# First image read flat for its statistics, two strips read once more, and early squares added on VectorE

## The chip, the cores and the metric

The kernel runs on one core of a Trainium2 chip. The metric is the device time of one execution in microseconds; the time of a kernel is the median of several runs. Profiles come from one profiled execution.

## The reference

Two residual blocks on eight images of 384 channels and 64 x 64 pixels, all in float32:

```
x = x + window_attention(group_norm(x))      # LayerNorm over channels, qkv, 8x8 windows, two branches
x = x + fft_feed_forward(group_norm(x))      # 1x1 conv, 8x8 real FFT filter, 3x3 depthwise conv, gated gelu, 1x1 conv

def group_norm(v):                           # 32 groups of 12 channels
    g = v.reshape(B, 32, 12, H, W)
    return ((g - mean(g, (2, 3, 4))) / sqrt(var(g, (2, 3, 4)) + 1e-5)).reshape(v.shape)
```

In the attention block the normalised image is normalised once more over the channels of each pixel (LayerNorm), then multiplied with the q, k and v weights. One branch of the heads attends in 8 x 8 windows, the other in windows shifted by four pixels. What matters here is the beginning: mean and variance of a group need the whole image before the first pixel can be normalised.

## The kernel before, in words

**Strips.** An image is worked on in eight strips of eight pixel rows. A strip is a tile of 128 partitions by 3 by 512 numbers (`strip`, 768 KB): partition p holds channels 3p to 3p+2, and each channel's eight rows of 64 pixels are 512 numbers, 2 KB in one piece in memory (`rows_of`, L67). Strips come into a ring of five buffers with the tag `x`.

**Order.** Every step of every strip is put on a list with a number that says when it is due (`at`, L260; the list at L693 to L773). The sorted list is handed to a scheduler, which may reorder instructions on an engine by its own estimates, but TensorE's matmuls stay in program order. Each engine takes its instructions in order, and so does each queue of transfers. Transfers of the steady part wait, by `in_dense_work` (L276), for a certain ScalarE instruction: the move of the first q tile out of PSUM (`qab`, L374) of the strip under way (`zs["gate"]`, L390).

**The start.** SyncE's queue issues, in this order: the eight strips of image 0 (`x_first`, L72 to L76: five in the `x` ring, three in the tiles `xn`, `ow` and `y2` that are not needed yet), the constants `cst` (L78), the raw q/k weights (`wqk_raw`, L96), and the weights `wv`, `wp`, `wi`, `wo`. ScalarE's queue issues 21 small transfers: vectors, q/k biases, filter tables. GpSimd issues 64 transfers of 2 KB for the position biases (`rpb_raw`, L154).

1. VectorE takes the statistics of each strip as it lands (`bn_stats`, L220), aggregates them (L227), and a small matmul with a constant matrix (`pm_a`, L230) averages over a group. A second one (`pv_a`, L241) leads to the standard deviation, by ScalarE and a reciprocal on VectorE (L243, L244).
2. VectorE copies the raw weights into their packed order (`pack_qk`, L114): twenty copies, and six on GpSimd, which gets odd blocks of the second branch only.
3. Strips are normalised on VectorE (`group_normal`, L308, three instructions each). The strips of image 0 that are in SBUF from the statistics (0, 1 and 2) are used from there; the rest of the image is loaded again when due (`load`, L282).
4. For the LayerNorm of a strip ScalarE squares it (`ln_square`, L313), GpSimd adds the three squares of a partition (L315, two additions of 512 numbers), and TensorE sums values and squares over the partitions (`ln_sums`, tile `ln`). Row statistics go through memory (`line`, `rs`, L336 to L338) and come back to scale the strip (L343).
5. Between the sums of strips 0 and 1 TensorE computes q/k bias products (`pb`) and centres the weights (`centre`, tile `pc`), with VectorE scaling them first (L181); then the same for v (`pv`, L181, `pc`) and for the second branch's q/k. After that the dense work starts: q/k tiles (`pq`), v (`pvv`), scores (`pS`), and so on.

TensorE's program order is thus: `pm_a`, `pv_a`, `ln` of strip 0, `pb` and `pc` of branch 0, `ln` of strip 1, `pv`, `pc` of v, `pb` and `pc` of branch 1, `pq`, ...

Of the kernel before, what the change touches and what calls it, by code (L numbers as in the profile page):

```python
# [9 lines left out]
ALU = mybir.AluOpType  # L10
# [3 lines left out]
KC = 3  # L14
# [3 lines left out]
ST = WS * SW  # L18
NS = SW // WS
# [13 lines left out]
def block_kernel(ctx: ExitStack, tc: tile.TileContext, out, x, consts, fsel, wqk, wv, bqk, bv,  # L33
                 wp, bp, lng, lnb, rpb1, rpb2, w_in, w_dw, w_out, filt):
    nc = tc.nc
# [22 lines left out]
    def strip(tag, bufs, name):  # L58
        return sb.tile([P, KC, ST], F32, tag=tag, bufs=bufs, name=name)
# [7 lines left out]
    def rows_of(img, s):  # L67

        return img[:, s * WS:(s + 1) * WS, :].rearrange("(p k) h w -> p k (h w)", k=KC)

    first_x = []
    for s in range(NS):  # L72
        tag, bufs = ("x", 5) if s < 5 else (("xn", 1), ("ow", 1), ("y2", 1))[s - 5]
        t = strip(tag, bufs, f"x_first{s}")
        nc.sync.dma_start(out=t, in_=rows_of(x[0], s))
        first_x.append(t)  # L76
    cst = cp.tile([P, N_CONST], F32, name="cst")
    nc.sync.dma_start(out=cst, in_=consts)  # L78
    ident = cst[:, C_ID:C_ID + P]
# [45 lines left out]
    for j, to, n, t, hp, of in blocks:  # L125
        nc.scalar.dma_start(out=bqk_sb[to:to + n].rearrange("p (b j) -> p b j", b=2)[:, :, j],
                            in_=bqk[of:of + n, 4 * t:4 * t + 4].rearrange("p (b i) -> p b i", b=2)[:, :, hp])
# [20 lines left out]
    for br, tab in ((0, rpb1), (1, rpb2)):  # L148
        raw = sb.tile([P, 2, 64], F32, tag="t2", bufs=3, name=f"rpb_raw{br}")
        raw_bias.append(raw)  # L150
        for h in range(4):
            half = slice(h % 2 * 64, h % 2 * 64 + 64)
            for y2 in range(WS):
                nc.gpsimd.dma_start(  # L154
                    out=raw[half, h // 2, y2 * WS:(y2 + 1) * WS],
                    in_=bass.AP(tab.tensor, h * 225 + y2 * 15, [[15, 8], [1, 8], [1, 8]]),
# [106 lines left out]
    xs, ys, y2s, qks, vs, os_, ots, x1s, zs = ({} for _ in range(9))  # L263
# [12 lines left out]
    def in_dense_work(i):  # L276


        if zs.get("gate"):
            behind(i, zs["gate"], mybir.DependencyClass.Sync, "transfer in dense work")  # L280

    def load(b, s, what):  # L282

        if b == 0 and (what == "stats" or what == "norm" and s < 3):
            xs[b, s, what] = first_x[s]
            return
        t = xs[b, s, what] = strip("x", 5, f"x_{what}_{b}_{s}")
        src = x1d[b][s] if what in ("mix", "finish") else rows_of(x[b], s)
        in_dense_work(nc.sync.dma_start(out=t, in_=src))
# [21 lines left out]
    def ln_square(b, s):  # L311
        sq = ys[b, s, "sq"] = strip("sq", 1, f"sq_{b}_{s}")
        nc.scalar.activation(sq, ys[b, s], AF.Square)  # L313
        for k in (1, 2):
            nc.gpsimd.tensor_tensor(sq[:, 0, :], sq[:, 0, :], sq[:, k, :], ALU.add)  # L315

    def ln_sums(b, s):

# [374 lines left out]
    for b in range(B):  # L693
        first = 2 * NS * b

        for s in range(NS):
            u = first - 14.84 + s if b else -10 + 0.1 * s
            at(u, load, b, s, "stats")
            at(u + (0.5 if b else 0.05), input_stats, b, s)
# [11 lines left out]
        for s in range(NS):  # L711
            u = first + 2 * s

            v = u - 4
            at(v - 0.84, load, b, s, "norm")
            at(v + 0.15, group_normal, b, s)
            at(v + 0.45, ln_square, b, s)
            at(v + 0.99, ln_sums, b, s)
            at(v + 1.35, ln_scale, b, s)
# [6 lines left out]
            for br in range(2):  # L726
                w = u + br
# [14 lines left out]
            else:  # L742
                places = [first + 2 * NS + f + (0.0 if s else 0.24) for f in (0.36, 0.44, 0.52)]
            at(int(places[0]) - 0.84, load, b, s, "add")
            for m in range(KC):
                at(places[m], project, b, s, m)
# [137 lines left out]
```

## Time and profile before

| what | us |
|---|---|
| median of 3 runs (3773.02 to 3777.32) | 3776.54 |
| the profiled execution: its time | 3773.36 |
| the profiled execution: its span | 3771.3 |
| TensorE busy | 3639.9 (97%) |
| VectorE busy | 2839.3 (75%) |
| ScalarE busy | 2379.7 (63%) |
| GpSimd busy | 438.2 (12%) |
| TensorE busy from 0 to 80 us | 28.6 |
| TensorE busy from 80 to 250 us | 168.5 |

All times within an execution count from the start of its span. TensorE's busy time is modelled from its matmuls; it says where TensorE works, not that it works at its best. The clock column of the stretches says which share of TensorE's full clock was granted.

### The profile page before, as it was taken

The page shows a single profiled execution, that of the slowest core. Times are in us where ns is not written, and L with a number is a line of the kernel's source. Part 1 is how long each engine was busy: PE and PEld are TensorE (multiplying, and loading weights), DVE is VectorE, ACT ScalarE, POOL GpSimd, SP SyncE. Part 2 cuts the span into 40 slices and gives each one's busy share as a digit, 9 for nine tenths or more (in the row PEclk, how much of TensorE's full clock was granted, in tenths as well). Part 3 has the DMA queues.
Part 4 walks back from the last instruction along what each step waited for, and adds up shares of the span by engine and source line. Part 5 has one row for each costly group of instructions (what it writes and reads, how often), then busy time and mean ns, then how long its engine had stood idle before and what let it go on. Part 6 is the DMA issues. An engine that isn't in the chain of part 4 may idle for free.

```text
span 3771.3 us, 88216 instructions
## 1 busy us (share of the span) xinstructions
PE 3639.9 (97%) x38144; PEld 2315.5 (61%) x38144; DVE 2839.3 (75%) x4601; ACT 2379.7 (63%) x3946; POOL 438.2 (12%) x776
## 2 busy tenths in 40 slices
PE   4999999999999999999999999999999999999898
PEld 2666666666666666666666656666666666666554
DVE  4554578777877687777887778877788777777898
ACT  1767676666676576665766756666676666676442
POOL 5111111111101011101101011111011111100000
PEclk9999999999999999999999999999999999999999
DMA  4222222323322233323332322322232222221422
GB/s 120 85 82 74 90 99 99 107 88 108 123 97 82 88 132 107 116 79 115 108 113 83 115 96 99 132 79 99 93 127 99 107 88 82 99 79 71 160 101 76
DMA packets 144488, 377.03 MB, mean 100 GB/s; under 512 B 12308, under 2 KB 12900, under 8 KB 144100
## 3 DMA queue, kind: packets, MB, share of 16 engines
q1 hardware_dynamic: 139952, 370.60, 27.9%
q8 instruction: 300, 4.92, 0.5%
q0 software_dynamic: 2048, 0.15, 0.1%
q10 hardware_dynamic: 2100, 0.63, 0.1%
q14 instruction: 88, 0.72, 0.1%
HBM read 270.54 MB, written 100.79 MB: 98 GB/s over the span
## 4 chain that ended last, share of the span: by engine, by line
PE 86%; DVE 5%; ACT 4%; issue 2%; DMA 2%; POOL 0%; ACTq 0%; DVEq 0%; POOLq 0%
PE pq L53 24%; PE pr L53 13%; PE pt L53 13%; PE pvv L53 12%; PE pw L53 6%; PE pS L53 3%; PE pA L53 3%; PE pz L53 3%; PE pT L56 3%; PE po L56 3%; DVE zz L653 2%; PE pf L53 2%; PE ln L53 2%; PE pc L53 1%; DMA rs<-line 1%
## 5 line engine op out<-in xcount | busy, mean ns | idle before, releaser
L653 DVE SCALAR_TENSOR_TENSOR zz<-z,dw_sb,zz 128x512 f32<-128x512 f32 x1490 | 1106.5, 761 | 189.3 <-ACT zz L647 166.5
L53 PE MATMUL pq<-y,wqk_sb 128*128 128x512 f32 x2160 | 990.3, 596 | 0.1
L53 PEld LDWEIGHTS pq<-y,wqk_sb 128*128 128x128 f32 x2160 | 402.8, 190 | 456.5 <-issue 424.7
L53 PE MATMUL pt<-wi_sb,xn 128*128 128x384 f32 x1536 | 535.2, 486 | 7.2 <-DVE x_finish L686 7.2
L53 PE MATMUL pr<-oT,wp_sb 128*128 128x512 f32 x1152 | 523.1, 592 | 1.0 <-DVE oT L517 1.0
L53 PE MATMUL pvv<-wv_sb,y 128*128 128x192 f32 x2880 | 496.0, 326 | 0.1
L53 PEld LDWEIGHTS pvv<-wv_sb,y 128*128 128x128 f32 x2880 | 471.6, 190 | 36.7 <-issue 23.4
L374 ACT ACTIVATE qab<-pq,bq_sb,cst 96x512 f32<-96x512 f32 (+1 forms) x256 | 198.0, 773 | 398.8 <-PE pq L53 397.1
L53 PEld LDWEIGHTS pt<-wi_sb,xn 128*128 128x128 f32 x1536 | 286.1, 190 | 212.9 <-issue 48.6
L374 ACT ACTIVATE kcd<-pq,vec 32x512 f32<-32x512 f32 x512 | 348.9, 681 | 9.0
L53 PEld LDWEIGHTS pr<-oT,wp_sb 128*128 128x128 f32 x1152 | 211.1, 190 | 224.4 <-issue 211.6
L356 POOL COPY y<-y 128x384 f32<-128x384 f32 x112 | 100.2, 895 | 1608.0 <-PE pvv L53 1108.2
L329 DVE TENSOR_TENSOR lr<-m 128x128 f32<-128x128 f32 x64 | 19.7, 308 | 318.3 <-ACT m L327 318.3
L647 ACT ACTIVATE zz<-z,dw_sb 128x512 f32<-128x512 f32 x183 | 133.9, 733 | 192.5 <-PE pw L53 187.0
L315 POOL TENSOR_TENSOR sq<-sq 128x512 f32<-128x512 f32 x128 | 167.4, 1308 | 634.3 <-ACT sq L313 629.3
L374 ACT ACTIVATE qcd<-pq,bq_sb,cst 96x512 f32<-96x512 f32 (+1 forms) x256 | 197.3, 771 | 43.9 <-PE pq L53 40.6
L526 DVE SCALAR_TENSOR_TENSOR x_add<-pr,vec,x_add 128x512 f32<-128x512 f32 x192 | 143.6, 748 | 105.6 <-PE pr L53 103.8
L564 ACT COPY t<-pt 128x384 f32<-128x384 f32 x256 | 124.9, 488 | 147.8 <-PE pt L53 145.0
L408 ACT COPY v<-pvv 128x384 f32<-128x384 f32 x256 | 121.2, 480 | 130.5 <-PE pvv L53 130.0
L53 PE MATMUL pw<-zz,wo_sb 128*128 128x512 f32 x384 | 181.9, 610 | 0.0
L374 ACT ACTIVATE kab<-pq,vec 96x512 f32<-96x512 f32 (+1 forms) x256 | 174.4, 681 | 9.0 <-PE pq L53 7.4
L449 ACT ACTIVATE e<-e 128x1024 f32<-128x1024 f32 x128 | 135.3, 1057 | 53.4 <-DVE e L443 52.0
(139 smaller groups left out, 5273.0 us busy)
## 6 DMA issues: line engine op xcount, KB each, us to landing
x_add<-in_x_dram SPq DMA_DIRECT2D x64, 768.0 KB
x1d<-x_add SPq DMA_DIRECT2D x64, 768.0 KB
x_mix<-x1d SPq DMA_DIRECT2D x64, 768.0 KB
x_finish<-x1d SPq DMA_DIRECT2D x64, 768.0 KB
out_dram<-x_finish SPq DMA_DIRECT2D x64, 768.0 KB
x_norm<-in_x_dram SPq DMA_DIRECT2D x61, 768.0 KB
x_stats<-in_x_dram SPq DMA_DIRECT2D x56, 768.0 KB
rs<-line SPq DMA_DIRECT2D x62, 256.0 KB
```

Source lines behind the costliest of these rows:

```text
L53: tc.keep_in_program_order(nc.tensor.matmul(*args, **kw))
L56: tc.keep_in_program_order(nc.tensor.transpose(*args, **kw))
L315: nc.gpsimd.tensor_tensor(sq[:, 0, :], sq[:, 0, :], sq[:, k, :], ALU.add)
L329: nc.vector.tensor_tensor(rc, m[:, 0:P], m[:, 0:P], ALU.mult)
L356: nc.gpsimd.tensor_copy(dst[:, :, :, :, 0:4], src[:, :, :, :, 4:8])
L374: return nc.scalar.activation(dst[to:to + n], pq[of:of + n], AF.Identity, bias=bias[of:of + n], scale=scale)
L408: nc.scalar.copy(v[:, 2 * g:2 * g + 2, :, 0:HD], pvv[:, 0:384].rearrange("p (g h d) -> p g h d", g=2, h=4))
L449: nc.scalar.activation(e, e, AF.Exp)
L526: nc.vector.scalar_tensor_tensor(t[:, m, :], pr, bp_sb[:, m:m + 1], t[:, m, :], ALU.add, ALU.add)
L564: nc.scalar.copy(t1, pt[:, 0:C])
L647: nc.scalar.activation(zz.rearrange("p (r c) -> p r c", c=SW), z[:, 1:9, 1:SW + 1], AF.Copy, scale=dw_sb[:, m, 4:5])
L653: i = nc.vector.scalar_tensor_tensor(acc.rearrange("p (r c) -> p r c", c=SW), z[:, dy:dy + 8, dx:dx + SW], dw_sb[:, m, TAPS[tap]:TAPS[tap] ...
```

## The change

The image is read for its statistics in eight flat parts: part i of partition p is the i-th piece of 6 KB of its three channels, one piece in memory instead of three rows of 2 KB. The statistics do not depend on which numbers of a channel group stand together. The parts lie in `xn`, `ow`, `y2`, `yw`, `sq` and three buffers of the `x` ring; the order of a flat part isn't that of a strip, so it can't be normalised from there. Strips 0 and 1 are read once more, into the other two buffers of the ring, ahead of the constants and weights on SyncE's queue. Strip 2 is no longer kept from the statistics and is loaded when due, like strips 3 to 7. The additions of squares of the first three strips of image 0 move from GpSimd to VectorE.

```diff
     first_x = []
-    for s in range(NS):
-        tag, bufs = ("x", 5) if s < 5 else (("xn", 1), ("ow", 1), ("y2", 1))[s - 5]
-        t = strip(tag, bufs, f"x_first{s}")
-        nc.sync.dma_start(out=t, in_=rows_of(x[0], s))
+    flat = x[0].rearrange("(p k) h w -> p (k h w)", k=KC)
+    for i in range(NS):
+        tag, bufs = (("xn", 1), ("ow", 1), ("y2", 1), ("yw", 1), ("sq", 1), ("x", 5), ("x", 5), ("x", 5))[i]
+        t = strip(tag, bufs, f"x_flat{i}")
+        nc.sync.dma_start(out=t.rearrange("p k c -> p (k c)"), in_=flat[:, i * KC * ST:(i + 1) * KC * ST])
         first_x.append(t)
+    norm_x = []
+    for s in range(2):
+        norm_x.append(strip("x", 5, f"x_norm_0_{s}"))
+        nc.sync.dma_start(out=norm_x[s], in_=rows_of(x[0], s))
     cst = cp.tile([P, N_CONST], F32, name="cst")
...
     def load(b, s, what):
 
-        if b == 0 and (what == "stats" or what == "norm" and s < 3):
-            xs[b, s, what] = first_x[s]
+        if b == 0 and (what == "stats" or what == "norm" and s < 2):
+            xs[b, s, what] = (first_x if what == "stats" else norm_x)[s]
             return
...
         for k in (1, 2):
-            nc.gpsimd.tensor_tensor(sq[:, 0, :], sq[:, 0, :], sq[:, k, :], ALU.add)
+
+            eng = nc.vector if b == 0 and s < 3 else nc.gpsimd
+            eng.tensor_tensor(sq[:, 0, :], sq[:, 0, :], sq[:, k, :], ALU.add)
```

## The prediction

> **What bounds the kernel now.** First the page: TensorE is busy for 97% of the span, so a change outside its work can only pay where TensorE stands still.
>
> ```profile
> PE 3639.9 (97%) x38144; PEld 2315.5 (61%) x38144; DVE 2839.3 (75%) x4601; ACT 2379.7 (63%) x3946; POOL 438.2 (12%) x776
> PE   4999999999999999999999999999999999999898
> POOL 5111111111101011101101011111011111100000
> ```
>
> Only the first of the forty slices (94 us each) has TensorE at 4 tenths, and there GpSimd has its highest digit. So I cut that slice into 20 us stretches; the columns are PE, PEld, DVE, ACT, POOL, clock, DMA share, GB/s.
>
> ```profile
> 20.00:40.00 20.00, 2.77 (x28) 1.61 (x28) 14.17 (x45) 1.75 (x2) 13.89 (x26) 1.00 1.03 319
> 40.00:60.00 20.00, 8.60 (x32) 5.72 (x32) 5.11 (x12) 2.16 (x3) 14.55 (x42) 1.00 0.08 6
> ```
>
> From 40 to 51 us everything rests except GpSimd, and the DMA engines have nothing to carry. The waits up to 100 us name the two stalls that matter:
>
> ```profile
> PE pm_a L53 <- DVE mv_a L227: 31.9, 1, 31.9
> DVE st L220 <- DMA x_first<-in_x_dram: 15.1, 8, 5.2
> PE ln L53 <- POOL sq L315: 14.7, 1, 14.7
> ```
>
> The first two are the read of the image for its statistics. The third is the one to look at: TensorE waits 14.7 us for the two additions of the first strip's squares on GpSimd. The chain of waits says why they are late:
>
> ```profile
> 41.20 6.63 POOL rpb_raw L154 x12
> 48.47 1.30 POOL sq L315
> 49.78 0.36 POOL wqk_sb L118 x2
> 50.13 1.23 POOL sq L315
> 51.40 0.66 PE ln L53 x8
> 52.06 3.93 PE pb L53 x18
> ```
>
> GpSimd issues the 64 small bias transfers first (until 47.8 us), then clears borders, and only then adds. ScalarE had the squares ready at 37.48 (L313: start 36.00, 1.48 long). Between 37 and 51 us TensorE is bound by a queue, not by data.
>
> **What the Trainium skill says.** (1) "SBUF — State Buffer", Who interferes with whom: a VectorE instruction with two SBUF inputs and a GpSimd instruction that reads SBUF exclude each other for a whole instruction. The trace agrees: L330 takes 1.26 us at 64.42, inside GpSimd's additions of 64.27 to 66.87, but 0.28 us at 57.11, after those of 53.96 to 56.72. (2) "DMA: Bandwidth & Descriptors", Issuing engines are not separate DMA queues: all share the same engines, so what stands ahead on SyncE's queue delays what follows. The trace agrees: the constants and weights came only after the strips. (3) The same page, Latency and other measured facts, has slower copies where rows lie at large power-of-two pitches; its pitches start at 512 KiB, ours are 16 and 48 KiB, so only the direction carries over. The trace shows it: two strips in 2 KB rows alone (116.9 to 122.6 us) moved at 273 GB/s, two in 6 KB runs (3554.9 to 3563.4) at 366. (4) "TensorE: Matmul & The Clock Gate", Part 1: the clock is halved until TensorE has been busy for a few microseconds. The trace agrees: 0.50 granted from 66 to 78 us.
>
> **Part 1: the additions on VectorE.** Removed from the path: the wait 36.68 to 51.40. Price of one: the nearest row is the 128x512 float32 addition from SBUF to SBUF at L670.
>
> ```profile
> L670 DVE TENSOR_TENSOR zz<-zz,zz 128x512 f32<-128x512 f32 x63 | 43.5, 690 | 5.7 <-DVE zz L653 0.5
> ```
>
> Two take 1.38 us instead of 2.6 on GpSimd. They queue on VectorE with the scaling of strips 0 and 1 (0.55 us an instruction) and the twenty weight copies at L118 (1.22 and 1.41 us in two groups).
>
> **Part 2: the transfers.** Flat parts have 6 KB runs. Estimate for one of 786 KB: 786/366 = 2.15 us, 0.15 added for the small transfers beside it, 2.3; bounds 2.15 and the present 3.2 (statistics of strips 1 to 4 started at 10.05, 13.07, 16.29, 19.53). First bytes move at 2.2 us. SyncE also waits to issue the strips (9.8 us behind the small q/k-bias transfers, 3.9 behind a strip); most is hidden behind strips in flight, and I leave 2 us exposed. Last part landed: 2.2 + 8 x 2.3 + 2 + 0.5 = 23.1 us, against 29.1 now. Its statistics (1.88) and the aggregate (0.8) are done by 26.
>
> But the two strips read again go ahead of the constants that the group mean multiplies with: 2 x 786/273 = 5.8 us, then 0.49 MB of constants, 1.4 us. The mean can start at 23.1 + 5.8 + 1.4 = **30.3**, against 31.94. So of the 6 us won by the flat read about 1.6 remain: what is late next is the constants. Bounds: 27 (2.15 us a part, no exposed wait) and 36.3 (3.2 a part). The q/k weights, 2 x 2.15 later, are in at 34.6, about as now (their copies ran from 35.89).
>
> **Part 3: the chain behind the mean.** From mean to strip 0 scaled takes 4.03 us (31.94 to 35.97): 34.3. Square: 35.9. VectorE meanwhile does the first copies and one scaling (1.8 us, to 36.1), then the additions, to 37.5. The last eight sums on TensorE start at 37.6 (51.40 now) and take 0.66. The q/k-bias products need the second group of copies, 37.5 + 1.41 = 38.9. They start at **38.9** instead of 52.06: 13.2 us. If VectorE's order has the additions behind all copies and scalings instead, about 2 us less.
>
> **Part 4: no more exclusion.** At 65.15 TensorE waits 1.99 us for `wv_sb`, because L330 (1.26 for 0.28) and the two L181 behind it (1.82 for 0.82) ran beside GpSimd's additions. These are gone: 1.9 us.
>
> **Part 5: strip 2.** It was in SBUF; now it has one load of its own, placed after the first q move, so SyncE holds it until ScalarE's `qab` (81.52 now, about 66.5 then) and it lands about 5.5 us later (issue 0.6, latency 2, transfer 2.9), at 72. Behind it on SyncE stand only the row statistics of strip 2, due after it anyway. VectorE's scaling (3 x 0.54) and additions (1.38) move into the dense part, 3.0 us, covered by VectorE's 10.85 us idle before 108.74; without that cover they would cost 3.0. ScalarE's square (1.48) moves from an idle place (62.71) to a stretch where ScalarE has 15 of 20 us busy: bounds 0 and 1.5, I take 0.7. TensorE asks for strip 2's sums at 107.26 now, about 93 then: 20 us of room behind the landing.
>
> GpSimd keeps six weight copies (0.35 us each) of the second branch only, now done near 50.5. TensorE needs them at 70.07 now, about 55 then. Hidden, with 4.5 us to spare.
>
> **Sum:** 13.2 + 1.9 - 0.7 = 14.4 us. The profiled execution took 3773.4 (span 3771.3): 3759.0. The runs' median, 3776.5, is 3.2 above that execution, and the forecast for the median is **3762**. What lies behind the start is relative to it: every later load is tied to work, so the shift carries to the end.
>
> **Rivals.**
> - **Flat is not faster** (as slow as rows, 3.2 us a part): mean at 36.3, everything behind it 6.0 later, q/k-bias products at 44.9, gain 7.2 + 1.9 - 0.7 = 8.4, time 3768. For it: SyncE's waits are not about run length. Against: the weights moved at 366 GB/s beside the same small transfers (34 to 36 us).
> - **GpSimd is late next.** If 6 KB packets held up the small bias transfers in the first 23 us to half their pace, GpSimd would finish some 9 us later, at 59.5, 4.5 past the 55 at which TensorE needs its copies: gain 10, time 3767. Against: they landed after 5.5 us beside the weights' longer packets, as beside the strips' (5.2 to 6.6).
> - **The stall changes its name.** If the first q/k-bias products waited for GpSimd's copies too, the gain would be 52.06 - 50.5 + 1.9 = 3.5, time 3773. Against: they started at 51.99 while the copies ran to 52.11, and the code gives GpSimd blocks of branch 1 only.
> - **The clock stays up.** Without the 2 us hole TensorE may keep its full clock over some of the 12 us of matmuls from 65 to 79; half of it, 6 us, is the most: 3756.
> - **Slower.** The extra load moves all later loads one place on in the ring of five `x` buffers. If this made loads of strips 3 to 63 collide, at 0.24 us a strip the gain is gone, and at 0.5 us it is 30 us: time 3792. For it: VectorE already waits 24.8 us in all for `x_stats` and 21.1 for `x_norm`. Against: each load still waits for the one five before it, as now.
>
> **Numbers.** Chances: forecast 0.60, clock 0.07, flat not faster 0.12, GpSimd 0.06, changed name 0.10, slower 0.05. A measurement here tells from no change about 0.2%, 7.5 us: below 3769.0 is faster. Of the middle rivals two thirds lie there: faster 0.79, same 0.16, slower 0.05. Range 3755 to 3771: the clock below, flat-not-faster with the runs' scatter of 4 us above; changed name and slower are left out.
>
> **What would show it.** Right: TensorE's wait for `sq` gone or under 3 us; two `sq` additions on VectorE near 0.69 us at 36 to 39; the last `x_flat` statistics before 26; TensorE's first mean released by the constants and not by `mv_a`; q/k-bias products near 39; dense work from about 64. Wrong: a new TensorE wait of over 5 us before 60 us, for weights or GpSimd; or idle TensorE time after 100 us grown by more than 5 us.

## The result and the profile after

| | before | after |
|---|---|---|
| median of 12 runs each, us | 3776.78 (3773.02 to 3777.95) | 3772.13 (3767.59 to 3776.19) |
| ratio of after to before, 95% interval | | 0.999 (0.9981 to 0.9999) |
| the profiled execution: time, span | 3773.36, 3771.3 | 3772.26, 3770.5 |

The change gains 4.65 us, with an interval of 0.4 to 7 us; the forecast was 14.4. The page of the kernel after, its busy times and its forty slices:

```profile
PE 3649.1 (97%) x38144; PEld 2321.9 (62%) x38144; DVE 2838.7 (75%) x4607; ACT 2377.5 (63%) x3946; POOL 430.6 (11%) x770
PE   5999999999999999999999999999999999999898
```

The first slice rose from 4 to 5 tenths, no more. What TensorE waits for up to 100 us, from the waits of the kernel after (engine, line, what it waited for: us in total, times, longest):

```profile
PE pm_a L53 <- DMA cst<-in_consts_dram: 34.0, 1, 34.0
DVE st L225 <- DMA x_flat<-in_x_dram: 13.9, 8, 4.3
PE ln L53 <- DVE sq L322: 4.9, 2, 2.8
PE pc L53 <- DVE wv_sb L186: 1.8, 1, 1.8
```

The wait of 14.7 us for GpSimd's additions is gone, as foreseen, and the mean is released by the constants. But it is released at 34.0, where `mv_a` had released it at 31.9; the wait for `sq` comes twice now; and the wait for `wv_sb` has stayed. The chain of waits of the kernel after shows these in order (start, length, what):

```profile
22.20 11.66 DMA cst<-in_consts_dram
...
33.99 0.57 PE pm_a L53 x2
...
41.48 0.66 PE ln L53 x8
42.14 3.93 PE pb L53 x18
...
49.65 1.35 DVE wqk_sb L190
51.00 0.61 DVE sq L322
...
51.64 0.70 DVE sq L322
...
53.13 3.72 PE pv L53 x24
```

The constants are issued at 22.20 and land 11.66 us later, behind two strips. The q/k-bias products start at 42.1, 9.9 us sooner than before; 13.2 were forecast. Then VectorE is on the path in places where it was not: strip 1's additions end at 52.34 and hold TensorE, and L350, the scaling of strip 0, stands between the v products and TensorE's next work. VectorE's timeline shows how strip 1 came so late:

```profile
47.31 0.10 DVE L199 TENSOR_TENSOR vec<-vec,pb 128x3 f32<-128x3 f32 x1
47.33 0.54 DVE L313 TENSOR_SCALAR y<-x_norm,gs_a 128x512 f32<-128x512 f32 x1
```

The third scaling of strip 1 runs at 47.33, behind work that needs `pb`. ScalarE squares at 48.11, and VectorE adds behind L190. A little later come the scalings of the v weights (`wv_sb`), which TensorE needs for `pc`. Before the change two of them stood directly behind L330, and the scaling of strip 0 (L343 there) behind them:

```profile
64.42 1.26 DVE L330 TENSOR_TENSOR lr<-m,lr 128x128 f32<-128x128 f32 x1
65.60 1.82 DVE L181 TENSOR_SCALAR wv_sb<-wv_sb,vec 128x384 f32<-128x384 f32 x2
67.34 1.75 DVE L343 TENSOR_TENSOR y<-y,rs 128x1536 f32<-128x1536 f32 x1
```

After it the scaling of strip 0 and a reciprocal stand ahead of these two:

```profile
56.95 0.28 DVE L337 TENSOR_TENSOR lr<-m,lr 128x128 f32<-128x128 f32 x1
57.15 1.75 DVE L350 TENSOR_TENSOR y<-y,rs 128x1536 f32<-128x1536 f32 x1
58.82 0.94 DVE L339 RECIPROCAL lr<-lr 128x128 f32<-128x128 f32 x1
59.68 0.73 DVE L186 TENSOR_SCALAR wv_sb<-wv_sb,vec 128x384 f32<-128x384 f32 x2
```

From before to after TensorE's program is the same instruction for instruction, and so is every engine's order behind the opening. So I compare three points of the opening in each trace: the mean (`pm_a`), the first q/k-bias product (`pb`) and the first q tile (`pq`), where the dense work begins. Starts are from TensorE's timeline; the forecast's are worked out from its own numbers (38.9 + 26.35 - 1.9 = 63.3, where 26.35 is the distance of before). The distance from `pb` to `pq` is split into the time in which TensorE works and the time in which it waits; the last column is the granted clock over it, in which the time ahead of a trace's first clock record counts as 1.00 (see the last section).

| us | mean | `pb` | first `pq` | `pb` to `pq` | busy | waits | clock |
|---|---|---|---|---|---|---|---|
| before | 31.94 | 51.99 | 78.34 | 26.35 | 23.6 | 2.7 | 0.76 |
| forecast | 30.3 | 38.9 | 63.3 | 24.4 | 23.6 | 0.8 | |
| after | 33.99 | 42.07 | 71.34 | 29.27 | 24.7 | 4.6 | 0.68 |
| after, a second execution | 36.08 | 44.30 | 71.63 | 27.33 | 22.2 | 5.1 | 0.75 |

At the first q tile 7.0 us are gained where 15.0 were forecast. Of the missing 8 us somewhat less than half is lost ahead of the mean, the rest between `pb` and `pq`. The experiments ask why.

Of the 7.0 us only 0.8 are left at the end of the two profiled executions (spans 3771.3 and 3770.5). In the kernel after, the products from 89.59 to 99 us ran mostly at half clock and took 9.7 us, 6.3 in its second execution. Besides, the trace of before was fast behind the opening: it took 3693.0 us from the first q tile to the end of its span, every other trace here 3695.6 to 3700.9. So the three points tell what happens in the opening, and the medians tell what the kernel gains.

### The profile page after: what moved, and what is told of

It reads as the page before. It is cut to its first block, busy times and chain, and to the rows that moved or that the text cites. A ratio compares the mean times of both kernels' runs of the same rounds, so it can differ in the third digit from the quotient of the medians.

```text
span 3770.5 us, 88221 instructions
## 1 busy us (share of the span) xinstructions
PE 3649.1 (97%) x38144; PEld 2321.9 (62%) x38144; DVE 2838.7 (75%) x4607; ACT 2377.5 (63%) x3946; POOL 430.6 (11%) x770
## 4 chain that ended last, share of the span: by engine, by line
PE 85%; DVE 6%; ACT 4%; DMA 3%; issue 2%; SPq 0%; ACTq 0%; DVEq 0%
PE pq L53 23%; PE pr L53 13%; PE pt L53 13%; PE pvv L53 12%; PE pw L53 6%; PE pS L53 3%; PE pz L53 3%; PE pA L53 3%; PE pT L56 3%; DVE zz L660 3%; PE po L56 2%; PE pf L53 2%; PE ln L53 2%; DMA rs<-line 1%; PE pc L53 1%
## 5 line engine op out<-in xcount | busy, mean ns | idle before, releaser
L322 POOL TENSOR_TENSOR sq<-sq 128x512 f32<-128x512 f32 x122 | 159.2, 1305 | 626.2 <-ACT sq L318 621.4
L381 ACT ACTIVATE kab<-pq,vec 96x512 f32<-96x512 f32 (+1 forms) x256 | 174.1, 680 | 11.8 <-PE pq L53 10.2
```

The source lines that it names most:

```text
L322: eng.tensor_tensor(sq[:, 0, :], sq[:, 0, :], sq[:, k, :], ALU.add)
L381: return nc.scalar.activation(dst[to:to + n], pq[of:of + n], AF.Identity, bias=bias[of:of + n], scale=scale)
```

## Experiments

Three theories. **Queue:** the flat parts are issued late, and two strips stand ahead of the constants. **Order:** without the long stall VectorE's order puts early strips' work ahead of the weights that TensorE waits for. **Clock:** TensorE runs parts of the opening at half clock. Each kernel was timed against the kernel before on one chip; the median of before was 3777.09 for the first four, 3777.91 for the next four, 3776.41 for the two kernels with two products and 3774.75 for the last one, so ratios are compared. Waits and clock are those between `pb` and the first `pq`, each from one trace.

| kernel | median, us | ratio, 95% interval | mean | `pb` | first `pq` | waits | clock |
|---|---|---|---|---|---|---|---|
| adds alone | 3771.4 | 0.9985 (0.9978 to 0.9991) | 31.16 | 39.18 | 70.66 | 5.9 | 0.69 |
| flat alone | 3774.61 | 0.9996 (0.9988 to 1.0004) | 35.45 | 51.98 | 73.37 | 0.7 | 0.87 |
| constants ahead | 3764.13 | 0.9967 (0.9955 to 0.998) | 31.36 | 40.74 | 63.19 | 1.9 | 0.85 |
| no bias loads | 3769.21 | 0.9981 (0.9971 to 0.999) | 32.53 | 40.62 | 66.29 | 3.9 | 0.82 |
| two queues | 3765.79 | 0.9968 (0.9955 to 0.998) | 28.16 | 39.97 | 62.98 | 1.7 | 0.85 |
| scaling later | 3769.63 | 0.9978 (0.997 to 0.9987) | 36.84 | 44.92 | 69.73 | 2.7 | 0.80 |
| five products | 3771.66 | 0.9985 (0.9979 to 0.9992) | 33.82 | 41.90 | 67.11 | 1.6 | 0.93 |
| three edits | 3763.76 | 0.9962 (0.9949 to 0.9974) | 26.06 | 39.82 | 62.80 | 3.1 | 0.87 |
| two products | 3772.26 | 0.9986 (0.9979 to 0.9993) | 33.40 | 41.47 | 69.29 | 3.4 | 0.76 |
| two products, scaling later | 3767.58 | 0.9979 (0.997 to 0.9989) | 33.90 | 41.98 | 67.42 | 1.1 | 0.80 |
| constants ahead, scaling later | 3758.01 | 0.9955 (0.9941 to 0.9968) | 30.53 | 39.89 | 62.73 | 1.9 | 0.88 |

### Each part alone

The kernel before with only the additions moved:

```diff
-            nc.gpsimd.tensor_tensor(sq[:, 0, :], ...)
+            eng = nc.vector if b == 0 and s < 3 else nc.gpsimd
+            eng.tensor_tensor(sq[:, 0, :], ...)
```

> One part alone: the squares of strips 0 to 2 added on VectorE, transfers as in the kernel before (strips read by rows, kept in SBUF). Theory 'transfers': the flat read with its two extra strips and the constants behind them costs the new kernel about 2 us at the mean (33.99 against 31.94) and nothing is gained by it, so this kernel starts its mean at 31.9, TensorE's last sums of strip 0 at 39 to 40 and the dense work (first pq) at 68 to 70, against 71.5 with the whole change: 2 us or more faster than the whole change, 5 to 10 us faster than before. Rival 'the additions are what costs': moving them to VectorE puts them ahead of other preparation, and first pq comes at 72 or later here too; gain over before under 4 us.

The whole change with the additions back on GpSimd:

```diff
-            eng = nc.vector if b == 0 and s < 3 else nc.gpsimd
-            eng.tensor_tensor(sq[:, 0, :], ...)
+            nc.gpsimd.tensor_tensor(sq[:, 0, :], ...)
```

> The other part alone: flat read, strips 0 and 1 read again, strip 2 loaded when due; the additions stay on GpSimd. Theory 'transfers': no gain, since TensorE waits for GpSimd's additions until about 51 to 52 as before (GpSimd's small transfers end at 48 or 49 either way); within 3 us of before, rather slower. Rival 'the flat read is worth something by itself': the mean or the first pq comes earlier than in the kernel before by over 2 us.

The additions alone give what the whole change gives (0.9985 against 0.999); their first q tile, at 70.66, lies between the two ranges expected. The flat read alone gives nothing that can be told from no gain in the medians. Its mean came at 35.45, released by the constants, and GpSimd's additions hold TensorE afterwards:

```profile
PE ln L53 <- POOL sq L321: 11.3, 1, 11.3
```

Its `pb` starts where before's does (51.98), yet its first q tile comes 5.0 us earlier, which had been named as the rival's sign. Of these 5.0 us 2.0 are waits, the rest TensorE's products at a higher clock (0.87 for 0.76).

With the additions alone `pb` starts at 39.18, and 12.8 us are gained there. Then TensorE waits for strip 1 twice, in the timeline of that kernel:

```profile
49.67 0.43 PE L53 MATMUL ln<-y,cst 128*32 128x128 f32 x8 [1.72 <-DVE y L308]
52.79 0.66 PE L53 MATMUL ln<-sq,cst 128*32 128x128 f32 x8 [2.69 <-DVE sq L316]
```

So the waits behind `pb` belong to the additions' part of the change, the late mean to the flat read's.

### The transfers

The constants ahead of the two strips:

```diff
+    cst = cp.tile([P, N_CONST], F32, name="cst")
+    nc.sync.dma_start(out=cst, in_=consts)
     norm_x = []
     for s in range(2):
...
-    cst = cp.tile([P, N_CONST], F32, name="cst")
-    nc.sync.dma_start(out=cst, in_=consts)
```

> The whole change, with the constants issued ahead of the two strips that are read again. Theory 'order of the queue': the mean waited for the constants alone, so it starts when the aggregate is ready, 30.6 to 31.5 instead of 33.99; strip 0 is then there by 32.5 to 33 and is scaled from 33 to 34 on (36.5 now): 2.5 to 3.5 us earlier at TensorE's last sums of strip 0 (38 to 39 instead of 41.5), and about as much at the end, 2 to 4 us, less or more by where the clock's windows fall. Rival: the weights, which land when they did, hold the q/k-bias products at 42, and nothing is gained.

The mean came at 31.36 and was released by the statistics, as expected. The dense work began at 63.19, and the median is 13 us below before's: 8 us less than the kernel after, where 2 to 4 were expected. The waits of this kernel up to 100 us:

```profile
PE pm_a L53 <- DVE mv_a L232: 31.4, 1, 31.4
PE ln L53 <- DVE sq L322: 2.7, 1, 2.7
...
PE pc L53 <- DVE wv_sb L186: 0.7, 1, 0.7
```

The mean explains only 2.6 us of the 8.2 at the first q tile. With the constants earlier the scheduler also ordered VectorE otherwise, strip 1's scaling ahead of the `pb` work and its additions at 46.10, and the second wait for `sq` is gone. Between `pb` and `pq` TensorE waits 2.6 us less than in the kernel after (1.9 for 4.6), and its products take 4.2 us less (20.5 for 24.7), at a clock of 0.85 instead of 0.68. Which part of this the order brought isn't shown.

The changed kernel without the 13 small q/k-bias transfers on ScalarE's queue; the q/k biases are zero in it:

```diff
-    for j, to, n, t, hp, of in blocks:
-        nc.scalar.dma_start(out=bqk_sb[to:to + n]..., in_=bqk[of:of + n, ...]...)
+    nc.vector.memset(bqk_sb, 0.0)
```

> The whole change, with the 13 small q/k-bias transfers on ScalarE's queue left out (the biases are set to zero by a memset instead). Theory 'SyncE is held at issue': the first five flat parts came 3.0 to 4.1 us apart because SyncE waited 13.3 us for these small transfers, the last three 2.3 us apart; without them all come about 2.3 us apart, the last lands near 22 to 23.5 instead of 27.9, and constants and weights come 4 to 5 us earlier: mean at 29 to 30, q/k-bias products at 37 to 38. Rival 'the flat reads themselves are slow (interference of small packets or memory)': parts still land over 3 us apart, mean later than 32.

The waits of SyncE's queue in the kernel after had pointed to them:

```profile
SPq L76 <- DMA vec<-in_bqk_dram: 13.3, 5, 4.6
```

SyncE waits for transfers of the other queue because, as the semaphore numbers in the traces show, the transfers of both queues take the same eight semaphores (counters that tell of a landing) in turn, and each issue waits until the last transfer with its semaphore has landed. The fourth part, issued at 10.08 in the kernel after, waited for the second of the bias transfers, which landed at 10.06.

Without the bias transfers the last part's statistics still began at 26.61 (27.89 with them), the first four 3.9 to 4.8 us apart: SyncE then waited 3.7 us for another small transfer (`lnb`) and 3.4 for a part. This expectation missed, and the rival's signs came, parts over 3 us apart at first and a mean later than 32 (32.53). But the edit also brought the filter tables forward (`fsel_sb` and `filt_sb` issued at 3.37 and 5.17, 16.35 and 16.99 with the bias transfers), so it doesn't decide. Half of the parts on the other queue, ahead of its small transfers, told more:

```diff
-        nc.sync.dma_start(out=t.rearrange("p k c -> p (k c)"), in_=flat[...])
+        queue = nc.scalar if i % 2 else nc.sync
+        queue.dma_start(out=t.rearrange("p k c -> p (k c)"), in_=flat[...])
```

> The changed kernel with flat parts 1, 3, 5 and 7 issued on ScalarE's queue ahead of its small transfers, the other four on SyncE's. If the statistics end late because SyncE issues the parts late (it stands 13.3 us behind small transfers): parts 2.2 to 2.5 us apart from the start, last one's statistics at 22 to 23.5 instead of 27.9, the constants 6.0 behind as now, mean at 28 to 29.5 instead of 33.99, q/k-bias products at 36.5 to 38, 4 to 5 us gained in the median: 3767 to 3768. If the small transfers themselves take the DMA engines' time in the first 16 us: last part at 26.5 to 28, mean at 32.5 to 34, median within 1.5 us of 3772.

From VectorE's timeline of this kernel (start, length, instruction, idle time before it):

```profile
7.11 3.66 DVE L226 BATCH_NORM_STATS2 st<-x_flat 128x6 f32<-128x512 f32 x6 [6.24 <-DMA x_flat<-in_x_dram]
...
21.17 3.66 DVE L226 BATCH_NORM_STATS2 st<-x_flat 128x6 f32<-128x512 f32 x6 [0.32 <-DMA x_flat<-in_x_dram]
```

And from ScalarE's:

```profile
21.17 10.73 ACTq L132 DMA_DIRECT2D vec<-in_bqk_dram  x13
...
33.41 0.26 ACT L249 ACTIVATE sd_a<-pv_a,eps_t 128x1 f32<-128x1 f32 x1 [29.76 <-DMA fsel_sb<-in_fsel_dram]
```

The parts come in pairs: one line is the statistics of two. The last pair's start at 21.17, so the last part's own near 23.0, and the mean starts at 28.16: both inside the expectation. From 5 to 22 us the DMA engines moved 351 GB/s, 228 in the kernel after. So the late statistics came from what was issued when, and the DMA engines could carry the image some 5 us sooner. How much of this is SyncE's wait and how much the small transfers' own time on the DMA engines isn't separated: here they were issued behind the parts. The expected start of `pb` (36.5 to 38) missed, at 39.97. The 13 bias transfers are now issued from 21.17 to 31.9 ahead of ScalarE's square root `sd_a`, which waits until 33.41 for a variance that was there at 30.1. A delay was moved from SyncE's queue to ScalarE's: now the small transfers waited for semaphores that the parts held.

### Order and clock

The profiled execution of the kernel after had TensorE at half clock in the v products (3.77 us for 2.20) and in twelve q products near 91 us (8.33 for 5.42). Another execution of the same kernel:

> The changed kernel unchanged, profiled in another execution. If the half clock belongs to the kernel's own holes: the 24 pv products near 53 us take 3.6 to 3.8 us again and the 12 pq products near 91 us 8.3. If it depends on how windows fall that run free of the kernel: at least one of the two is at 2.2 or 5.4. Landing of the constants: 33.8 to 34.2 if the transfers repeat, up to 37 if they scatter as between the earlier runs.

Both were at full clock (2.17 and 5.42); only the half clock in `pb` of the second branch is in both, and in the kernel before (3.84 in each). The totals differ by 1.2 us (3771.07 and 3772.26), and the first q tile is at 71.63 and 71.34. The granted clock in both, from the stretches of TensorE (stretch, length, busy time, clock, DMA share, GB/s), first the execution of the kernel after:

```profile
53.00:57.00 4.00, 4.00 (x29) 0.50 0.02 4
62.00:66.00 4.00, 4.00 (x18) 0.50 0.26 66
```

And the second execution:

```profile
53.00:57.00 4.00, 2.40 (x32) 1.00 0.13 44
62.00:66.00 4.00, 4.00 (x17) 0.50 0.27 66
```

So where the half clock falls is not a property of the kernel alone. The mean, released by the constants, starts at 36.08 here. In seven executions with this same opening of SyncE's queue (these two, the flat read alone, and the four kernels with a later scaling or added products below) it starts between 33.4 and 36.8.

VectorE's order: the scaling of strip 0 by its row statistics behind that of the v weights.

```diff
-            at(v + 1.35, ln_scale, b, s)
+            at(v + 1.35 if b or s else -0.93, ln_scale, b, s)
```

> The changed kernel with the scaling of strip 0 by its row statistics (L350, 1.75 us) put behind the v weights' scaling on VectorE; every other order before 60 us is as in the changed kernel. If VectorE's order kept the 1.9 us of part 4 from coming: TensorE's wait of 1.82 us for wv_sb falls under 0.5 us, the gain behind it is 8.3 to 9 us instead of 7.0, median 3770 to 3771. If the wait comes from the half clock of the pv products alone: it stays at 1.5 to 1.9 us, and the median at 3772.

TensorE's timeline of this kernel:

```profile
55.83 0.43 PE L53 MATMUL ln<-sq,cst 128*32 128x128 f32 x8 [2.07 <-DVE sq L322]
56.19 3.65 PE L53 MATMUL pv<-vec,wv_sb 128*128 128x1 f32 x24
59.70 3.90 PE L53 MATMUL pc<-wv_sb,cst 128*128 128x384 f32 x6
```

VectorE now scales the v weights first:

```profile
60.15 0.74 DVE L186 TENSOR_SCALAR wv_sb<-wv_sb,vec 128x384 f32<-128x384 f32 x2
60.81 0.95 DVE L339 RECIPROCAL lr<-lr 128x128 f32<-128x128 f32 x1
61.67 1.70 DVE L350 TENSOR_TENSOR y<-y,rs 128x1536 f32<-128x1536 f32 x1
```

No wait for `wv_sb` is left between `pv` and `pc`, though `pv` was at half clock: the order kept the wait alive, not the clock. (The reciprocal L339, 0.95 us, moved behind the scalings as well.) From `pb` to the first q tile it takes 24.81 us, for 29.27 and 27.33 in the kernel after; the forecast had 24.4. Its mean happened to come late (36.84).

The clock: five products of constants in TensorE's wait for strip 1, then two.

```diff
         for to, t, n in ((0, ys[b, s], KC), (P, ys.pop((b, s, "sq")), 1)):
+            if to and b == 0 and s == 1:
+                pd = psum("pd")
+                for _ in range(5):          # 2 in the second kernel
+                    matmul(pd, ones_c, cst[:, 0:ST], start=True, stop=True)
```

> The changed kernel with five products 128x512 of constants (unused result, about 2.2 us at full clock) in TensorE's 2.07 us wait ahead of strip 1's last sums. VectorE's order shifts by one: the scaling of strip 0 now stands ahead of all three v weight scalings. If TensorE's idle time ahead of 52.4 us brings the half clock: the 24 pv products take 2.2 us instead of 3.77, the clock is full at 52 to 56; the 12 pq products near 90 us take 5.4 if their window was a consequence, 8.3 if it has its own cause (the thin pv, pb and pp products before it). Median 3768.5 to 3771. If the one-column products themselves bring it, pv stays at 3.8 and the median at 3772 to 3773.

> The changed kernel with two products 128x512 of constants (unused result, four passes of 0.46 us) in TensorE's 2.07 us wait ahead of strip 1's last sums; all other engines' orders are the changed kernel's. If that hole brings the half clock: pv takes 2.2 us and the sums start no later than 0.2 us behind the changed kernel's; the wait for wv_sb grows to about 3 us if VectorE's order alone sets it, or stays at 1.8 if it moves up with pv (the v weights' scaling waits for pv); first pq products at 16.0 to 17.0 us behind the sums of strip 1 instead of 19.07; median 3768 to 3771. If the hole does not matter: pv 3.8, median 3772.

Five were too many: each takes two passes of 0.456 us, 4.56 us in all, which I had taken for 2.2, and VectorE's order shifted with them. With two, which leave all other orders alone, TensorE's timeline shows:

```profile
49.97 1.98 PE L53 MATMUL pd<-cst 128*128 128x512 f32 x4
52.11 0.43 PE L53 MATMUL ln<-sq,cst 128*32 128x128 f32 x8 [0.16 <-DVE sq L322]
52.47 2.17 PE L53 MATMUL pv<-vec,wv_sb 128*128 128x1 f32 x24
...
58.09 2.93 PE L53 MATMUL pc<-wv_sb,cst 128*128 128x384 f32 x4 [2.47 <-DVE wv_sb L186]
```

The v products are at full clock, the wait for `wv_sb` grows to 2.47 us, and the half clock begins at 55.7, in that wait. The median is that of the kernel after (3772.26 and 3772.13), where 3768 to 3771 were expected if the hole mattered; five products, with the v products at full clock too (2.17 us), gave 3771.66. At the first q tile these two kernels are 2.1 and 4.2 us ahead of the first execution of the kernel after, but their medians don't show it, within intervals of some 3 us. So full clock in the v products alone doesn't bring the missing 8 us.

The clock isn't out of the account, though. In the tables the traces with the longest waits between `pb` and `pq` (4.6 us and more) have the lowest clock (0.68 to 0.75), and those with waits under 2 us have 0.80 to 0.93. That shorter waits bring the higher clock is likely but not shown. Both edits together:

> Both: the two products in the hole, and strip 0's scaling by its row statistics behind the v weights' scaling on VectorE. If clock and order are separate losses: from the sums of strip 1 to the first pq products 14.0 to 15.0 us instead of 19.07 in the changed kernel and 13.9 in the one with the order alone (its pv at half clock); median 3766 to 3769. If they are one loss: the same as the better of the two alone, 3769 to 3770.

From `pb` to `pq` it takes 25.44 us, with no wait for `wv_sb`. The first q tile comes 14.1 us behind the sums of strip 1 and the median is 3767.58, both in the ranges for separate losses; but the ratio of 0.9979 is that of the order alone (0.9978), so a gain from the clock isn't shown. The median is 4.7 us below that of the two products alone, timed with the same runs of before. The two intervals overlap, but twice the edit of the order has pointed the same way, and the traces show the wait that it removes.

### Together

Constants ahead, parts on two queues, scaling later:

> Constants issued ahead of the two re-read strips, flat parts on two queues, and strip 0's scaling behind the v weights. If the three delays are separate: last flat statistics at 23 to 24.5, mean at 26 to 28 (released by the statistics, not by the constants), then the strips and q/k weights are next (landed by 31 and 35): q/k-bias products at 37 to 39, no wait over 0.5 us for wv_sb, median 3758 to 3762. If the q/k weights bound it, the products stay at 40 to 41 as with the constants ahead alone (40.74), and the median at 3763 to 3765.

The mean came at 26.06, released by the statistics as expected, but `sd_a` again stood behind ScalarE's bias transfers (`y` at 34.19), `pb` at 39.82 fell between the two ranges expected, and the median (3763.76) is that of the constants alone, outside the 3758 to 3762 expected for separate delays. Eight us won ahead of the mean are lost to one queue. Without the second queue:

> Constants ahead of the two re-read strips, and strip 0's scaling by its row statistics behind the v weights' scaling; all flat parts on SyncE. If the constants' place already removed the loss behind the mean (32 us from mean to first pq there, 0.67 us left of the wait for wv_sb): mean at 31 to 33.5, first pq products 31 to 32 us behind it, median 3763 to 3765, as with the constants alone. If order and transfers add up as separate losses: 3760 to 3762.

At 3758.01 this is the fastest, better than before and after, and below both ranges expected. Its trace is of the slowest of its five runs (3763.72), and the first q tile there (62.73) is only 0.5 us ahead of that with the constants alone (63.19). Its ratio 0.9955 (0.9941 to 0.9968) overlaps that of the constants alone, so whether the later scaling adds 4 us there stays open.

## Why the prediction was wrong

**Right.** The cause of the 14.7 us was right, and so was that they would go: two additions of 0.69 and 0.68 us on VectorE stand where the wait for GpSimd was. The constants were late next, as forecast. The chain behind the mean was right: `pb` comes 8.1 us after it, 8.6 forecast. GpSimd's weight copies ended at 50.31 (50.5 forecast), and nobody waited for them. Strip 2's load was issued at 76.46, VectorE waited 6.0 us for it until 81.28, and TensorE not at all. TensorE's idle time behind 100 us is unchanged: of 3671 us it worked 3592.5, 3591.2 before. None of the signs named for being wrong came either; the loss sits in a late mean and in waits of about 2 us each, under the 5 us that would have counted as a sign.

**Wrong, first step: part 2, "8 x 2.3" and "I leave 2 us exposed".** The last three parts did come 2.3 us apart, at 23.3, 25.6 and 27.9. Those before came 3.0 to 4.1 apart, while SyncE's waits to issue grew from 9.8 to 13.3 us. The last part was in at 27.9, not at 23.1, which is 4.8 us. With all parts issued ahead of the small transfers the statistics of the last pair started at 21.2: the order of issue is what cost it. Against this the constants came 6.0 us behind the last part, not 7.2. I had priced the two strips by 273 GB/s, a mean over a stretch in which two transfers begin and end. In the middle of that stretch the same rows moved at 357 (stretch, length, TensorE busy, clock, DMA share, GB/s):

```profile
116.90:122.60 5.70, 5.70 (x29) 1.00 0.76 273
117.60:121.40 3.80, 3.80 (x19) 1.00 0.98 357
```

The 366 beside it is such a mean too, over four transfers (3.10 MB) and not two. In the kernel after the two strips and the constants, 2.07 MB, took 6.0 us, some 345 GB/s. Sum: +3.7 us at the mean. The rule that I cited from the Trainium skill, "DMA: Bandwidth & Descriptors", on large pitches was the wrong one to lean on: its Specifications call 512 B enough for the full rate, and the traces nearly side with that, 357 GB/s in 2 KB rows against 366 from 22 to 28 us of the kernel after, where flat parts in 6 KB runs landed. The flat read thus saved little transfer time; what it cost was the second read of two strips.

**Wrong, second step: all that lies between `pb` and the dense work "as before", less part 4's 1.9 us.** It takes 29.3 and 27.3 us in the two executions, for 24.4 forecast: 4.8 and 2.9 us more. The waits are longer in both, 4.6 and 5.1 us where the forecast left 0.8. The products took 1.1 us more than before in the first execution and 1.4 us less in the second, with the half clock at other places. So the waits are what failed, by some 4 us, and the difference between the two executions is the products' time at the clock that each was granted.

Part 4 had the exclusion right: L337 takes 0.28 us at 56.95 for 1.26 before. But it took the wait of 1.99 us to be the price of that exclusion alone. Where the exclusion went, L350 stood ahead of two of the three v scalings, and 1.8 of the wait stayed (2.3 in the second execution); moving L350 and the reciprocal behind it removed the wait. The other part is the new wait of 2.07 us for strip 1, in both executions. The stall of 14.7 us had been cover for strip 1's scaling and square; I had asked what of the removed wait's own chain is late next, and not what else had been done under it. That strip 1 is late by VectorE's order is shown only indirectly: with the constants ahead the scaling stood early and the wait was gone, but the mean was earlier too.

Together 3.7 - 0.5 + 4.8 = 8.0 us of the 15.0 at the dense work. The rest, from 7.0 us in the trace to 4.65 in the medians, is within the interval.

**The rivals.** The nearest time was that of "The stall changes its name" (3773), but nothing of it came: nobody waited for GpSimd's copies, and the agreement is chance. "Flat is not faster" (3768) came nearest in what happened. It said 3.2 us a part, and the statistics of the eight parts started 3.2 us apart on average, (27.89 - 5.18)/7; it named SyncE's waits, and these grew. Its mean of 36.3 stands against 33.99 and 36.08. GpSimd was late for nobody, and the later loads did not collide. "The clock stays up" did not come either: from `pb` to `pq` the clock was 0.68 and 0.75, 0.76 before.

As a limit the sum is near what can be reached: with the constants ahead or with two queues the kernels began the dense work at 62.7 to 63.2, and their medians are 3758 to 3766. But they got there by another way, and the agreement with 63.3 is in part luck. Their `pb` starts later than forecast (39.8 to 40.7), and TensorE's products between `pb` and `pq`, at 0.85 to 0.88 of the clock, take 20 to 21 us where the sum had kept 23.6.

## What to carry to other kernels

When a long stall is removed, list what the other engines did under it, not only what the stalled engine waits for next: that work now stands in an engine's queue ahead of the next critical step, and its place there has to be set. A read that is faster per byte gains nothing if the queue that issues it stands waiting, or if the bytes that it adds go ahead of a small transfer on which the first computation depends. Take a transfer's rate from a stretch in which the DMA engines are busy throughout: the same rows showed 273 GB/s with their start and end counted in, and 357 without.

## What the runs showed of the hardware

The half clock comes in stretches whose lengths are multiples of 3.4 us in every trace (3.4, 6.8, 10.2, 13.7 and 20.5, but for one cut off by the end), at places that differ between executions of one kernel. This agrees with the Trainium skill, "TensorE: Matmul & The Clock Gate", Part 1, which describes a free-running window of 3.4 us. What I had not expected is that thin products, 24 of one column that keep TensorE "busy" for all of a stretch (53 to 57 us in the first execution), run there at 0.50 of the clock.

The clock's records begin late, at 62.1 us in the kernel before and at 49.0 in the kernel after. For the time ahead of them the views print 1.00, and that is no measurement. The 24 sums of a strip took 1.57 us at 37.10 in the kernel after and 0.86 at 49.54, and the first 18 `pb` products took 4.00 us in every trace, where the 18 of the second branch took 2.06 at full clock with the constants ahead. So TensorE's first products ran at about half speed, before and after alike.

And with the same opening transfers the mean started between 33.4 and 36.8 us in seven executions, most of the whole effect under study: a mean's start is not known from one trace to better than that.
